# Layer 0's normed input turned to channels through DRAM, as planes of half words, in place of TensorE transposes

## The chip, the cores and the metric

The kernel runs on one core of one Trainium2 chip. A core has five engines that run side by side, each taking its instructions in order: TensorE (PE in the profile, with PEld for its weight loads), VectorE (DVE), ScalarE (ACT), GpSimd (POOL) and SyncE (SP, which here only issues DMAs). The metric is the device time of one execution in microseconds. Before the change it is 2533.7 us, the median of three runs (2533.55 to 2534.89).

## The reference

64 graphs of 256 nodes with 256 features pass two layers. Layer 0 is a gated graph network, layer 1 a graph attention layer:

```python
# layer 0
h = jnp.maximum(_layernorm(x, axis=-1), 0.0)
A = (adj != 0)
for i in range(3):
    m = jnp.einsum('bnd,de->bne', h, weight[i])
    aggr = jnp.einsum('bst,bsd->btd', A, m)
    h = _gru_cell(aggr, h, w_ih, w_hh, b_ih, b_hh)
x = x + h
# layer 1
h = jnp.maximum(_layernorm(x, axis=-1), 0.0)
h = (h @ W.T + b).reshape(B, N, 4, 64)
logits = leaky_relu(l_src[:, :, None, :] + l_dst[:, None, :, :], 0.2)
probs = softmax(where(adj == 1, logits, NEG_INF), axis=2)
x = x + einsum('bijh,bjhc->bihc', probs, h)
```

The change concerns the first line of layer 0 alone: its result is wanted in two layouts, nodes on the partitions (for the aggregation) and channels on the partitions (for the gates).

## The kernel before

The 64 graphs go through in 32 pairs. A pair has 512 rows (two graphs of 256 nodes), kept as four blocks of 128 rows; `x`, `xn` and the adjacency hold rows on the partitions, `hT_a`, the state of the gated network, holds the 256 channels as two blocks of 128 partitions with 512 nodes each.

There is no loop that the hardware schedules. The program is written out by `plan`: `at(tick, phase, p, fn)` files a piece of code under a tick and one of three phases, and at the end all pieces are emitted by tick, then by phase (STEP, READY, REST), and within a phase with the later pair first. Each engine executes its own instructions in that order and waits on semaphores for the others. A piece that stands early in the order and waits holds up everything behind it on its engine.

A pair starts at tick t0 = 18 p. Its three steps of the gated network take six ticks each, at t0 + 0, t0 + 12 and t0 + 24, so that in the steady state each tick has exactly one step piece, from one of three pairs in flight: modulo 18, ticks 0 to 5 belong to the first step of the newest pair, ticks 6 to 11 to the third step of the pair two before, ticks 12 to 17 to the second step of the pair one before. When ticks are numbered below, they are meant modulo 18. The rest, layer normalisation, layer 1, loads and stores, is filled in between as READY and REST pieces. Layer 1 of a pair runs up to tick t0 + 66, so up to four pairs are in work at once.

The pieces of one step that matter here: `tick_3` ends on VectorE with the sum that starts the bank `pe` (L479), `tick_4` has `first_n` (L495), which VectorE writes into the bank `pn0`, and `tick_5` starts with the product that TensorE adds into that bank (`input_n`, L500, recorded at L312). TensorE's product must wait for VectorE's `first_n`.

The input of layer 0 is made like this (times relative to t0):

- `plan_norm` (L329): statistics at -14 and -13, the reciprocal deviation on GpSimd at -13, the normed rows `xn_a` by four VectorE instructions (L351) at -7.
- `plan_relu_T` (L360): at -4 and at -3, four TensorE transposes each (L370) into a bank of PSUM and one ScalarE relu (L371) out of it into `hT_a`.
- `first_hi` and `first_lo` (L740, L744) at -3: the relu of `xn_a` split in a rounded part `hNhi` on ScalarE (L742) and the remainder `hNlo` on VectorE (L746).
- `state_sums` (L401) at -1: differences of `hT_a` on VectorE.

Around these ticks VectorE also has the maxima of layer 1 (L899), the statistics of the second layer normalisation (L339), the shift `top` (L908 to L910) and the last steps' updates (L527, L528), all in the order of the plan. Another DMA transpose is there already: `linked` (L863) brings the mask of layer 1 turned out of DRAM, issued on SP at t0 + 36, behind a write of the same data at t0 + 35 (L803).

Buffers are named by tag in `BUFS`: a tag with n buffers is handed out n times before the first is reused. `row` has four, of which the rows of scores (`drow_0`, `drow_1`, L856) use two per pair; the first four uses are for `hh_T` and two of the message weights.

Of the kernel before, what the change touches and what calls it, by code (L numbers as in the profile page):

```python
# [9 lines left out]
F32 = mybir.dt.float32  # L10
F32R = mybir.dt.float32r
BF16 = mybir.dt.bfloat16
I32 = mybir.dt.int32
AF = mybir.ActivationFunctionType
ALU = mybir.AluOpType
# [2 lines left out]
P = 128  # L18
# [8 lines left out]
def gated_gnn_then_gat_kernel(  # L27
# [39 lines left out]
    nc = tc.nc  # L67
    B, N, D = x.shape
    L = weight.shape[0]
# [3 lines left out]
    KD = D // P  # L73
    KN = N // P
    PB = 2
    R = PB * KN
    T = PB * N
# [10 lines left out]
    dram = ctx.enter_context(tc.tile_pool(name="rows", bufs=2, space=bass.MemoryType.DRAM))  # L88
# [8 lines left out]
    def bank(name):  # L97
        return ps_m.tile([P, 512], F32, tag="mm", name=name)

    BUFS = {  # L100
        "x": 5, "adj": 2, "edge": 2, "noedge": 2, "hT_a": 2, "xn": 2, "val": 2, "row": 4, "zz": 4, "o": 2,
    }

    def buf(tag, shape, name, dtype=F32):
        return sb.tile(shape, dtype, tag=tag, name=name, bufs=BUFS.get(tag, 1))
# [6 lines left out]
    def load_adj(p, name):  # L112
        at = buf("adj", [P, R, N], f"{name}_{p}", I32)
        nc.sync.dma_start(at, adj_rows[ts(p, T), :].rearrange("(r q) t -> q r t", q=P))
        return at
# [10 lines left out]
    def load_gates(name, src):  # L126
        nat = buf("zz", [P, G, D], f"{name}_nat")
        for g0 in range(0, G, 3):
            nc.sync.dma_start(
                nat[:, g0 : g0 + 3, :], src[g0 * P : (g0 + 3) * P, :].rearrange("(g q) d -> q g d", q=P)  # L130
            )
        return nat

    def load_square(tag, name, src):
        y = buf(tag, [P, KD, D], name)
        nc.sync.dma_start(y, src.rearrange("(k q) e -> q k e", q=P))
        return y
# [5 lines left out]
    hh_T = [buf("row", [P, G * P], f"hh_T_{k}") for k in range(KD)]  # L143
    w_msgs = [load_square("Z", "w_msg_0", weight[0])]
    ih_nat = load_gates("ih", w_ih)
    w_msgs += [load_square("row", f"w_msg_{l}", weight[l]) for l in range(1, L)]
    w_nat = load_square("zz", "w_nat", W)
    bi = const.tile([P, G], F32, name="bi")
    bh = const.tile([P, G], F32, name="bh")
# [5 lines left out]
    make_identity(nc, ident)  # L155
    ident16 = const.tile([P, P], BF16, name="ident16")
    nc.vector.tensor_copy(ident16, ident)
# [144 lines left out]
    def flat(y):  # L302
        return y.rearrange("q r d -> q (r d)")
# [17 lines left out]
    STEP, READY, REST = range(3)  # L321
# [4 lines left out]
    def at(tick, phase, p, fn):  # L326
        plan.setdefault(tick, ([], [], []))[phase].append((-p, fn))

    def plan_norm(src, name, p, ticks):  # L329

        v = {}

        def stats(r0):
            def fn():
                if not v:
                    v["st"] = small.tile([P, R, 6], F32, tag="st", name=f"st_{name}")
                    v["mv"] = small.tile([P, R, 2], F32, tag="mv", name=f"mv_{name}")
                for r in (r0, r0 + 1):
                    nc.vector.bn_stats(v["st"][:, r, :], src()[:, r, :])  # L339
                    nc.vector.bn_aggr(v["mv"][:, r, :], v["st"][:, r, :])  # L340
            return fn

        def deviation():
            rstd = v["rstd"] = small.tile([P, R], F32, tag="rstd", name=f"rstd_{name}")
            nc.vector.tensor_scalar_add(rstd, v["mv"][:, :, 1], EPS)
            nc.gpsimd.tensor_tensor(rstd, rstd, mhalf, ALU.pow)

        def result():
            xn = v["xn"] = buf("xn", [P, R, D], f"xn_{name}")
            for r in range(R):  # L350
                nc.vector.tensor_scalar(  # L351
                    xn[:, r, :], src()[:, r, :], v["mv"][:, r, 0:1], v["rstd"][:, r : r + 1],
                    op0=ALU.subtract, op1=ALU.mult,
                )

        for t, fn in zip(ticks, (stats(0), stats(2), deviation, result)):
            at(t, READY, p, fn)
        return v

    def plan_relu_T(v, tag, name, p, ticks):  # L360

        w = {}

        def fn(k):
            def go():
                if not w:
                    w["hT"] = buf(tag, [P, KD, T], f"hT_{name}")
                pt = bank(f"pt_{name}_{k}")
                for r in range(R):
                    nc.tensor.transpose(pt[:, ts(r, P)], v["xn"][:, r, ts(k, P)], ident)  # L370
                nc.scalar.activation(w["hT"][:, k, :], pt, AF.Relu)  # L371
            return go

        for k, t in enumerate(ticks):
            at(t, REST, p, fn(k))
        return w

    def by_c(y):
# [184 lines left out]
    def plan_tail(t0, p, v, g, turn_back, residual):  # L563
# [6 lines left out]
        def links():  # L570
            v["link"] = buf("hNhi", [P, PB, KN, N], f"link_{p}", BF16)
            for i in range(PB):
                pt = ps_m.tile([P, KN, N], BF16, tag="mm", name=f"plink_{p}_{i}")
                for j in range(KN):
                    for s in range(KN):
                        nc.tensor.transpose(pt[:, j, ts(s, P)], v["noedge"][:, i * KN + s, ts(j, P)], ident16)
                nc.vector.tensor_scalar_mul(v["link"][:, i, :, :], pt, 1 / 16)
# [132 lines left out]
    def plan_pair(p):  # L710
        t0 = APART * p
        v = {}
# [3 lines left out]
        def ready(t, fn):  # L716
            at(t0 + t, READY, p, fn)
# [14 lines left out]
            v["edge"] = buf("edge", [P, R, N], f"edge_{p}", F32R)  # L732
            nc.vector.tensor_scalar(v["edge"], v["adj"], 0.0, None, op0=ALU.not_equal)

        xn_a = plan_norm(lambda: v["x"], f"a{p}", p, [t0 - 14, t0 - 13, t0 - 13, t0 - 7])
        ready(-1 if p else -2.5, to_edge)
        h = plan_relu_T(xn_a, "hT_a", f"a{p}", p, [t0 - 4, t0 - 3])


        def first_hi():  # L740
# [37 lines left out]
        for l in range(L):  # L778
            end = last and l == L - 1
            g = Step(f"{p}_{l}", l, lambda: h["hT"], end)  # L780
            t = 2 * SUB * l
# [15 lines left out]
        def bar():  # L797

            v["noedge"] = buf("noedge", [P, R, N], f"noedge_{p}", BF16)
            nc.vector.tensor_scalar(v["noedge"], v["adj"], 1.0, 16 * MASKED, op0=ALU.not_equal, op1=ALU.mult)  # L800
            if not last:
                v["noedge_rows"] = dram.tile([R, P, N], BF16, tag="noedge", name=f"noedge_dram_{p}")
                nc.sync.dma_start(v["noedge_rows"].rearrange("r q t -> q r t"), v["noedge"])  # L803
# [3 lines left out]
        if last:  # L807
            plan_tail(t0, p, v, g, lambda i: turn_back(L - 1, i), residual)
            return
        xn_b = plan_norm(lambda: v["x"], f"b{p}", p, [t0 + 32, t0 + 33, t0 + 33, t0 + 34])  # L810
        hb = plan_relu_T(xn_b, "hT_b", f"b{p}", p, [t0 + 35, t0 + 36])

        def values(r0):
# [37 lines left out]
        rows, drow, logits = {}, {}, {}  # L851
# [11 lines left out]
        def linked():  # L863

            v["link"] = buf("link", [P, KN, T], f"link_{p}", BF16)
            nc.sync.dma_start_transpose(v["link"], v["noedge_rows"].rearrange("r q t -> (r q) t"))
# [59 lines left out]
        for y in range(R * H // 2):  # L926
            r, h0 = divmod(2 * y, H)
# [36 lines left out]
    for p in range(NPAIR):  # L964
        plan_pair(p)
# [52 lines left out]
```

## Time and profile before

| | |
|---|---|
| median of three runs | 2533.7 us |
| the profiled execution | 2540.86 us |
| its span, first to last instruction | 2539.1 us |
| granted TensorE clock, mean | 0.995 |
| period of a pair in the steady state | 76.94 us |
| transposes of `pt_a` (L370) | 256, in 64 groups of four |
| evictions of `pt_a` (L371) | 64, 0.59 us each |
| `xn_a` (L351) | 128 instructions, median 403 ns |
| DMA engines | 251.91 MB moved, mean 99 GB/s |

The page gives busy times and shares of each engine over the span; the chain is the sequence of work that ended last, followed back from the last instruction. A line of the timeline reads: start in us, length in us, engine, source line, operation, output from inputs, shapes, count, and in brackets how long the engine idled before it and who released it. Neighbouring instructions of one engine overlap a little (VectorE's by some 0.08 us), so that the distance between two starts is what an instruction costs its queue. A line of the waits reads: who waited, for whom, us in total, how many times, the longest.

### The profile page before, as it was taken

What the parts mean: (1) busy time and instruction counts of PE and PEld (TensorE: products, weight loads), DVE (VectorE), ACT (ScalarE), POOL (GpSimd) and SP (SyncE); (2) the same over time, 40 slices, a digit from 0 to 9 for tenths busy, and PEclk for the clock granted to TensorE, in tenths of its full rate; (3) what the DMA queues carried; (4) which work ended last, traced back from release to release, by engine and by line L of the source; (5) the groups of instructions that cost most, each with busy time, mean ns of one, the idle gap of its engine ahead of it and who ended that gap; (6) DMA issues with size and microseconds to landing.
All of it is one profiled execution on the core that took longest, in us unless ns stands there. A gap on an engine that the chain in (4) does not pass through costs nothing.

```text
span 2539.1 us, 38539 instructions
## 1 busy us (share of the span) xinstructions
PE 2514.5 (99%) x13918; PEld 2246.4 (88%) x13918; DVE 1824.1 (72%) x4458; ACT 1466.2 (58%) x3095; POOL 645.5 (25%) x514
## 2 busy tenths in 40 slices
PE   8999999999999999999999999999999999999998
PEld 6888898888889888989888988888988889898887
DVE  5567777677777777776777776777777777767667
ACT  3456565565555565555665655655656656556664
POOL 0122232222222222323232323222222223222221
PEclk9999999999999999999999999999999999999998
DMA  3033434553435544345544444534344544354443
GB/s 94 17 74 88 97 93 108 109 125 92 92 92 117 109 113 99 87 95 117 117 100 93 98 102 109 125 92 100 88 113 109 119 95 93 87 124 110 93 95 89
DMA packets 168223, 251.91 MB, mean 99 GB/s; under 512 B 42896, under 2 KB 128352, under 8 KB 168032
## 3 DMA queue, kind: packets, MB, share of 16 engines
q0 software_dynamic: 33728, 130.03, 26.6%
q1 hardware_dynamic: 132736, 119.41, 16.0%
q8 instruction: 110, 1.80, 0.3%
q14 instruction: 81, 0.66, 0.1%
q10 hardware_dynamic: 1568, 0.01, 0.0%
HBM read 215.62 MB, written 25.67 MB: 95 GB/s over the span
## 4 chain that ended last, share of the span: by engine, by line
PE 97%; DVE 1%; DMA 1%; ACT 1%; issue 0%; POOL 0%; SPq 0%; DVEq 0%
PE pd L312 20%; PE pn L312 13%; PE pc L312 13%; PE po L542 9%; PE pa L440 7%; PE qb L418 6%; PE pe L312 6%; PE p L312 6%; PE qa L418 5%; PE pv L820 4%; PE pback L770 3%; PE pt_a L370 1%; PE pt_b L370 1%; PE pc L238 1%; DVE any L899 0%; DMA hh_nat<-in_L_gnn_w_hh_dram 0%
## 5 line engine op out<-in xcount | busy, mean ns | idle before, releaser
L510 POOL TENSOR_TENSOR R<-hT_a,hn 128x512 f32<-128x512 f32 x191 | 317.8, 1664 | 879.4 <-ACT hn L506 821.5
L312 PE MATMUL pn<-aggr,w_a 128*128 128x256 f32 x1536 | 367.1, 382 | 0.0
L312 PE MATMUL pd<-T,w_a 128*128 128x256 f32 x1536 | 366.3, 381 | 0.0
L312 PEld LDWEIGHTS pn<-aggr,w_a 128*128 128x128 f32 x1536 | 287.0, 190 | 43.1 <-DVE pn L495 6.4
L312 PEld LDWEIGHTS pd<-T,w_a 128*128 128x128 f32 x1536 | 287.9, 191 | 37.6
L542 PEld LDWEIGHTS po<-val,zz 128*128 128x128 f32 x2048 | 250.3, 195 | 4.5
L542 PE MATMUL po<-val,zz 128*128 128x65 f32 x2048 | 247.2, 275 | 0.0
L899 DVE CUSTOM_DVE_ANT_0 any<-drow,noedge 128x256 f32<-128x256 f32 x496 | 236.9, 478 | 9.8 <-DMA drow<-score_dram 1.0
L506 ACT ACTIVATE hn<-pn,bi 128x256 f32<-128x256 f32 x384 | 160.3, 469 | 144.3 <-PE pn L312 144.2
L425 ACT ACTIVATE R<-pc,brz 128x256 f32<-128x256 f32 x192 | 80.5, 470 | 278.5 <-PE pc L312 278.5
L527 DVE SCALAR_TENSOR_TENSOR R<-Z,R 128x512 f32<-128x512 f32 x192 | 131.8, 687 | 147.6 <-POOL R L510 142.8
L558 POOL TENSOR_TENSOR x<-x,o 128x256 f32<-128x256 f32 x124 | 112.0, 904 | 481.6 <-DVE o L553 481.6
L761 DVE TENSOR_TENSOR hNlo<-pback,hNhi 128x512 fp32r<-128x512 f32 x128 | 88.4, 691 | 201.6 <-ACT hNhi L760 201.6
L919 ACT ACTIVATE zz<-zz,val 128x256 f32<-128x256 f32 x496 | 224.9, 509 | 0.0
L495 DVE SCALAR_TENSOR_TENSOR pn<-R,hn 128x512 f32<-128x512 f32 x192 | 142.5, 742 | 93.7 <-ACT hn L421 77.2
L425 ACT ACTIVATE R<-pe,brz 128x256 f32<-128x256 f32 x192 | 80.5, 470 | 185.9 <-PE pe L312 185.9
L528 DVE SCALAR_TENSOR_TENSOR hT_a<-R,hn 128x512 f32<-128x512 f32 x192 | 174.6, 909 | 14.3 <-ACT m5n L446 1.4
L312 PE MATMUL pd<-T,w_h 128*128 128x256 f32 x768 | 181.5, 379 | 0.0
L312 PE MATMUL pc<-aggr,w_a 128*128 128x256 f32 x768 | 181.5, 379 | 0.0
L312 PE MATMUL pe<-aggr,w_a 128*128 128x256 f32 x768 | 181.4, 379 | 0.0
L312 PE MATMUL pc<-hT_a,w_h 128*128 128x256 f32 x768 | 181.4, 379 | 0.0
L312 PE MATMUL p<-T,w_a 128*128 128x256 f32 x768 | 181.4, 379 | 0.0
(176 smaller groups left out, 5258.5 us busy)
## 6 DMA issues: line engine op xcount, KB each, us to landing
zz<-score_dram POOLq DMA_DIRECT2D x62, 1024.0 KB, 11.7
zz<-topT_dram POOLq DMA_DIRECT2D x62, 1024.0 KB, 8.7
adj<-in_adj_dram SPq DMA_DIRECT2D x64, 512.0 KB
drow<-score_dram SPq DMA_DIRECT2D x62, 512.0 KB
x<-in_x_dram SPq DMA_DIRECT2D x32, 512.0 KB
out_dram<-x SPq DMA_DIRECT2D x31, 512.0 KB
noedge_dram<-noedge SPq DMA_DIRECT2D x31, 256.0 KB
score_dram<-score SPq DMA_DIRECT2D x124, 4.0 KB
```

The costliest lines, as they stand in the source:

```text
L312: nc.tensor.matmul(pt[:, ts(c, N)], w[:, k, j * D + c * P : j * D + (c + 1) * P], src[:, k, :], start=start and c == 0 and k == 0, stop=(c ...
L418: nc.tensor.matmul(pt, w_n[:, j, :], src, start=start, stop=True, skip_group_check=True)
L425: nc.scalar.activation(of(dst, i)[:, c, :], src[:, c, :], AF.Tanh, bias=brz[:, g0 + c : g0 + c + 1], scale=0.5)
L440: nc.tensor.matmul(pt[:, ts(i, N)], hN[half][:, i * KN + s, ts(e, P)], edge[:, i * KN + s, :], start=(s == 0 and half == 0), stop=(s == KN ...
L495: nc.vector.scalar_tensor_tensor(by_c(self.bank(f"pn{i}")), of(self.R, i), 1.0, of(self.hn, i), op0=ALU.add, op1=ALU.mult)
L506: nc.scalar.activation(n__[:, c, :], p_n[:, c, :], AF.Tanh, bias=bi[:, 2 * KD + c : 2 * KD + c + 1])
L510: nc.gpsimd.tensor_sub(of(self.R, i), of(self.hT(), i), n__)
L527: nc.vector.scalar_tensor_tensor(d_, of(self.Z, i), 1.0, d_, op0=ALU.add, op1=ALU.mult)
L528: nc.vector.scalar_tensor_tensor(of(self.hT(), i), d_, 0.5, of(self.hn, i), op0=ALU.mult, op1=ALU.add)
L542: nc.tensor.matmul(po[:, ts(h_, VC)], zz[:, j, h_, ts(s, P)], v["val"][:, i * KN + j, ts(h_, VC)], start=(j == 0), stop=(j == KN - 1),)
L899: nc.vector.tensor_tensor_reduce(any_, drow[r // KN][:, h, :], v["noedge"][:, r, :], 1.0, -3.0e38, ALU.add, ALU.max, accum_out=v["top"][:, ...
L919: nc.scalar.activation(zz[:, h, :], zz[:, h, :], AF.Prelu, alpha=ALPHA, bias=v["val"][:, r, S0 + H + h : S0 + H + h + 1],)
```

## The change

For pairs 2 to 31 the turned input no longer comes from TensorE. The normed rows are made three ticks earlier (-10 in place of -7) and put through the relu in place by ScalarE. `plan_turn` then takes them to channels in three pieces: `halve` at -9 copies the 32-bit words on VectorE into two planes of 16-bit half words (low halves, high halves, 256 each to a row) and writes them to DRAM; `turn` at -8 reads them back with one DMA transpose[...], so that each plane arrives with channels on the partitions; `join` at -3 puts low and high halves side by side again on VectorE, into `hT_a`. Both DMAs are issued on SP. To make room, the tag `row` goes from four buffers to two, and the message weights of steps 1 and 2 are loaded into the tag `noedge`.

```diff
-        "x": 5, ..., "row": 4, "zz": 4, "o": 2,
+        "x": 5, ..., "row": 2, "zz": 4, "o": 2,
...
-    w_msgs += [load_square("row", f"w_msg_{l}", weight[l]) for l in range(1, L)]
+    w_msgs += [load_square("noedge", f"w_msg_{l}", weight[l]) for l in range(1, L)]
...
+    def plan_turn(src, tag, name, p, ticks):
+        w = {}
+
+        def halve():
+            words = buf("words", [P, R, 2, D], f"words_{name}", U16)
+            nc.vector.tensor_copy(words.rearrange("q r w d -> q r d w"), src().bitcast(U16).rearrange("q r (d w) -> q r d w", w=2))
+            w["rows"] = dram.tile([R, P, 2 * D], U16, tag="words", name=f"words_dram_{name}")
+            nc.sync.dma_start(w["rows"].rearrange("r q e -> q r e"), words.rearrange("q r w d -> q r (w d)"))
+
+        def turn():
+            w["turned"] = buf("turned", [P, 2, KD * T], f"turned_{name}", U16)
+            nc.sync.dma_start_transpose(
+                w["turned"].rearrange("q w (k n) -> q (w k) n", k=KD), w["rows"].rearrange("r q e -> (r q) e")
+            )
+
+        def join():
+            w["hT"] = buf(tag, [P, KD, T], f"hT_{name}")
+            nc.vector.tensor_copy(
+                flat(w["hT"]).bitcast(U16).rearrange("q (n w) -> q n w", w=2), w["turned"].rearrange("q w n -> q n w")
+            )
+
+        at(ticks[0], READY, p, halve)
+        at(ticks[1], REST, p, turn)
+        at(ticks[2], READY, p, join)
+        return w
...
-        xn_a = plan_norm(lambda: v["x"], f"a{p}", p, [t0 - 14, t0 - 13, t0 - 13, t0 - 7])
+        dma_a = p >= 2
+        norm_ticks = (-14, -13, -13, -10) if dma_a else (-14, -13, -13, -7)
+        xn_a = plan_norm(lambda: v["x"], f"a{p}", p, [t0 + t for t in norm_ticks])
         ready(-1 if p else -2.5, to_edge)
-        h = plan_relu_T(xn_a, "hT_a", f"a{p}", p, [t0 - 4, t0 - 3])
+        if dma_a:
+            ready(-10, lambda: nc.scalar.activation(flat(xn_a["xn"]), flat(xn_a["xn"]), AF.Relu))
+            h = plan_turn(lambda: xn_a["xn"], "hT_a", f"a{p}", p, [t0 - 9, t0 - 8, t0 - 3])
+        else:
+            h = plan_relu_T(xn_a, "hT_a", f"a{p}", p, [t0 - 4, t0 - 3])
```

Of the program's order: TensorE loses 60 rows of four transposes and nothing else moves in it; VectorE gets `halve` and `join`, both directly behind the `pe` sum (L479) of their tick, and `xn_a` earlier; ScalarE gets the relu in tick 8 and loses two evictions in ticks 14 and 15; GpSimd's order is unchanged; SP gets the write and the transpose of a pair ahead of the output write of an earlier one.

More of the change, by code (lines that the diff above doesn't have):

```diff
@@ L12 @@
 BF16 = mybir.dt.bfloat16
+U16 = mybir.dt.uint16
 I32 = mybir.dt.int32
@@ L100, in gated_gnn_then_gat_kernel @@
     BUFS = {
-        "x": 5, "adj": 2, "edge": 2, "noedge": 2, "hT_a": 2, "xn": 2, "val": 2, "row": 4, "zz": 4, "o": 2,
+        "x": 5, "adj": 2, "edge": 2, "noedge": 2, "hT_a": 2, "xn": 2, "val": 2, "row": 2, "zz": 4, "o": 2,
     }
```

## The prediction

> **What bounds the kernel now.** I read the page first: busy shares, then the chain that ended last. TensorE is busy for 99% of the span and makes 97% of the chain; the transposes that the change removes stand in that chain with 1%.
>
> ```profile
> PE 2514.5 (99%) x13918; PEld 2246.4 (88%) x13918; DVE 1824.1 (72%) x4458; ACT 1466.2 (58%) x3095; POOL 645.5 (25%) x514
> ...
> PE 97%; DVE 1%; DMA 1%; ACT 1%; issue 0%; POOL 0%; SPq 0%; DVEq 0%
> ```
>
> A share of 72% for VectorE is an average over stages, so I looked next at TensorE's timeline over one steady pair of graphs (its period is 1094.32 - 1017.38 = 76.94 us, and its pattern repeats), around the two groups of L370:
>
> ```profile
> 1054.34 0.60 PE L370 MATMUL pt_a<-ident,xn_a 128*128 128x128 f32 x4
> 1054.78 0.60 PE L770 MATMUL pback<-ident,hT_a 128*128 128x128 f32 x4
> ...
> 1058.67 0.60 PE L370 MATMUL pt_a<-ident,xn_a 128*128 128x128 f32 x4
> 1059.11 0.60 PE L418 MATMUL qb<-T4n,w_n 128*128 128x256 f32 x2
> ...
> 1062.99 0.27 PE L837 MATMUL ptopT<-ident,top 128*16 128x128 f32 x1
> 1063.10 1.98 PE L312 MATMUL pn<-aggr,w_a 128*128 128x256 f32 x8
> ```
>
> A group of four transposes holds TensorE for 0.44 us (start to next start, 1054.78 - 1054.34), not the 0.60 of its own pipelined length. The `pn` product that follows at 1063.10 needs `first_n` (L495) from VectorE. The same stretch on VectorE:
>
> ```profile
> 1046.09 0.18 DVE L551 RECIPROCAL rden<-po 128x4 f32<-128x4 f32 x1 [2.20 <-PE po L542]
> ...
> 1057.56 0.69 DVE L479 TENSOR_TENSOR pe<-pd,m 128x512 f32<-128x512 f32 x1
> 1058.16 0.41 DVE L339 BATCH_NORM_STATS2 st_b<-x 128x6 f32<-128x256 f32 x1
> ...
> 1059.84 0.24 DVE L910 TENSOR_SCALAR top<-top,barred 128x16 f32<-128x16 f32 x1
> 1060.69 1.22 DVE L746 SCALAR_TENSOR_TENSOR hNlo_a<-xn_a,hNhi_a 128x1024 fp32r<-128x1024 f32 x1 [0.61 <-ACT hNhi_a L742]
> 1062.33 0.70 DVE L495 SCALAR_TENSOR_TENSOR pn<-R,hn 128x512 f32<-128x512 f32 x1 [0.42 <-ACT hn L421]
> ```
>
> VectorE waits for TensorE at 1046.09 and then runs without a gap worth the name until 1060: 13.28 of the 14.00 us are busy in the view by stretches, the rest is between instructions. Its only slack before `first_n` is 0.61 + 0.42 us, both waits for ScalarE. `first_n` ends at 1063.03, `pn` starts at 1063.10. The waits of the weight loads say the same for nearly every pair:
>
> ```profile
> PEld pn L312 <- DVE pn L495: 6.4, 30, 0.2
> ```
>
> So in this stretch two engines are bound at once, TensorE and a queue on VectorE that is anchored to the end of the fourth output product at 1045.9. Elsewhere VectorE has room: it idles 5.3 us in 1023 to 1040.
>
> [...] the first pair's `link` transpose (256 KB, issued at 153.93 with nothing beside it) keeps the DMA engines 0.63 busy over 155 to 157, which is 1.26 us or some 208 GB/s. [...] L733 agrees for the first (1024 elements in 676 ns, against 681 ns for the 512 of L404). [...] No instruction in this trace hops so, and the cost of the change turns on it.
>
> **The change part by part.** It touches pairs 2 to 31, 30 of 32.
>
> *TensorE, removed:* 2 groups of 4 transposes a pair, 0.435 us each: 0.87 us a pair, 30 x 0.87 = 26.1 us. All of it is on the bounding engine.
>
> *ScalarE:* 2 evictions of 0.59 us go from ticks 14 and 15; one relu over 1024 columns comes in tick 8 at about 1.06 us (L742 has that shape). In sum nothing, but the place matters. The relu waits for `xn_a`, which VectorE now makes in tick 8, and the exponentials (1.07) and the `hNhi` cast (0.59) are queued behind it.
>
> *VectorE, moved:* `xn_a` (4 instructions, 1.4 us at the 403 ns of one) moves from 1040.36 to 1027.1.
>
> *VectorE, added:* `halve` in tick 9 behind L479, `join` in tick 15 behind L479. Both are copies of 2048 half words, one side of each hopping between two planes. Below: 2048 at L733's rate (0.52 ns each and 0.14 fixed) is 1.2 us. [...] At one element a cycle as in L404: 2.3 us. [...] I take 1.9[...]; 1.2 and 3.7 stay as ends. Nothing below 1.2 is expected[...].
>
> *Place of `halve` (H):* `xn_a` ends at 1028.5, relu 1029.6, exponentials 1030.5, `hNhi` 1031.0 (it ended at 1029.0); `hNlo`, two output instructions and L479 then end at 1032.9, before TensorE wants it at 1033.74. `halve` runs 1032.9 to 1032.9 + H; the state sums, maxima and one output (2.8 us) follow, and `first_n` ends at 1036.3 + H. TensorE wants it at 1038.93, so H up to 2.6 us costs nothing; above, the surplus per pair. At 1.9 it is hidden by the idle time that VectorE had there and by the place that `xn_a` left.
>
> *Place of `join` (J):* the queue from 1058.16 to `top` (1.8 us) now starts after it, so `hNlo_a` can start at 1059.9 + J, `first_n` 1.14 later, and it ends at 1061.8 + J. The waits for ScalarE are gone, since ScalarE loses two evictions and TensorE's inputs to it come 0.4 to 0.9 earlier. `pn` starts at 1061.83 + J instead of 1063.10: a change of J - 1.27 us, and never better than the -0.87 that TensorE saves. Behind `first_n` all follows shifted, as TensorE waits with it, and the 1.17 us that VectorE idles at 1069.35 absorb the remainder. With J = 1.9 this is +0.63 us a pair. It holds for pairs 3 to 31: when pair 2 is prepared, no maxima run yet and VectorE idles 1.50 us at 144.38, so that pair gains 0.87.
>
> *DMA and queues:* a write of 512 KB at 1035 (the output of the same size: issued 1048.03, moved 1049.0 to 1050.5) lands by about 1038; the transpose is twice `link`: issue 2 x 1.24, moving 2 x 1.26, so landed by about 1045, and `join` wants it at 1058. The DMA engines move nothing between 1034 and 1045. On SP both stand ahead of the output write of 1048, which waits for GpSimd anyway; the loads of `x` and `adj` come behind that. Cost nothing, with 13 us to spare. GpSimd's queue has no change.
>
> *`row` from 4 buffers to 2, `w_msg` in `noedge`:* the rows of a pair are loaded at 1088 and last read by the maxima at 1057 of the cycle before; nothing.
>
> Sum: 29 x 0.63 - 0.9 = +17.4 us. The profiled execution took 2540.86 us (span 2539.1 and 1.8 around), 0.28% over the median of 2533.7; the difference is carried to the median unscaled: 2551.
>
> **Rivals.**
> 1. *The join is a plain two-a-cycle copy, the hop free* (J = 1.2). Then 29 x -0.06 - 0.9 = -2.6 us, 2531: the saving on TensorE turns wholly into a wait. For it: L733[...].
> 2. *One element a cycle* (J = H = 2.3): 29 x 1.01 - 0.9 = +28.4, 2562. With the hop besides (3.7): 29 x 2.43, and H beyond 2.6 by 1.1 at the first `pn`, 29 x 1.1: +101.5, 2635.
> 3. *TensorE stays alone in front* (the faster side). Place: `pn` in tick 17 of the schedule. It needs `first_n` no later than TensorE, which is J below 1.27; full 26.1 us come at J = 0.40 (2508). [...] For it: 99% against 72%. Against: the gapless stretch, which a mean over the span hides.
> 4. *The transpose lands late* and VectorE waits at `join`. It needs 13 us more than twice `link`; each microsecond beyond costs 29 us. Nothing in the profile speaks for it but that planes of half words were not moved before.
>
> **How the numbers follow.** This kernel's runs tell a change from none at about 0.2%, 5 us. Forecast (J near 1.9) 0.38; rival 1 0.20, of which 0.15 within 5 us and 0.05 below; rival 2 at 2562 0.20 and at 2635 0.07; rival 3 0.10; rival 4 0.05. Slower 0.70, same 0.15, faster 0.15. The range leaves out rival 3 and the far end of 2 and 4: 2526 to 2590.
>
> **What would show it.** Right: L370 for `pt_a` down from 256 to 16; `join` near 1.9 us on VectorE with no gap before `first_n`; waits of TensorE for `first_n` of about 1.5 us (0.87 + 0.63) in some 29 places; TensorE's busy share lower; no wait at `join` for DMA. Wrong: a gap on VectorE before `first_n`; a `join` of 1.2 us or less; waits of `pn` in tick 10 (then `halve` is too long); a DMA wait at `join`.

## The result and the profile after

The changed kernel takes 2654.8 us (median of four runs, 2649.7 to 2659.0) against 2534.1 for the kernel before: ratio 1.0475, 95% interval 1.0453 to 1.0498. The forecast was 2551 with a range up to 2590, so the sign was right and the size was not: +121 us in place of +17. The execution in the profile took 2659.0 us, its span was 2656.9 and its mean granted clock 0.982 (0.995 before). Runs of one kernel fall into two groups some 6 us apart by the mean clock that they were granted (for the kernel before 0.998 or more, or about 0.995), so differences under 5 us are not read, and "at like clock" below means that only runs of 0.998 or more are compared.

The page of the changed kernel, busy shares and the shares of the chain that ended last:

```profile
PE 2537.9 (96%) x13678; PEld 2249.5 (85%) x13678; DVE 1977.3 (74%) x4518; ACT 1475.2 (56%) x3065; POOL 655.5 (25%) x514
...
PE 58%; DVE 33%; ACT 6%; issue 2%; DMA 1%; POOL 0%; DVEq 0%; SPq 0%; ACTq 0%
```

TensorE executes 240 matmuls fewer and is yet busy for 23 us longer, and VectorE now makes a third of the chain. Both are explained in what follows. The instruction groups of the two new copies (count, then duration in ns as minimum, median, maximum):

```profile
L386 DVE COPY words_a<-xn_a x30: 5372/5604/5629, 122.0 to 2454.9; 128x2048 uint16<-128x2048 uint16 x30
...
L398 DVE COPY hT_a<-turned_a x30: 1216/1218/1220, 147.6 to 2484.7; 128x2048 uint16<-128x2048 uint16 x30
```

Both move 2048 half words per partition. `halve` (L386) reads them in order and writes each to the other plane than the last one: 5.60 us, 2.7 ns each. `join` (L398) reads each from the other plane and writes them in order: 1.22 us, 0.6 ns each. VectorE's timeline in one steady pair shows what 5.6 us do to its queue (`...` marks lines left out):

```profile
1164.08 0.69 DVE L508 TENSOR_TENSOR pe<-pd,m 128x512 f32<-128x512 f32 x1
1164.68 5.61 DVE L386 COPY words_a<-xn_a 128x2048 uint16<-128x2048 uint16 x1
1169.86 0.95 DVE L433 TENSOR_TENSOR T<-hT_a 128x512 f32<-128x512 f32 x1
...
1172.73 0.69 DVE L524 SCALAR_TENSOR_TENSOR pn<-R,hn 128x512 f32<-128x512 f32 x1
```

There is no bracket of idle time on any of these lines: VectorE runs through, and the `pn` of tick 11 (L524) ends at 1173.42. TensorE's timeline, first around `pn` of tick 17 of the pair before, behind `join`, then around this `pn`:

```profile
1117.15 0.27 PE L873 MATMUL ptopT<-ident,top 128*16 128x128 f32 x1
1118.04 1.99 PE L313 MATMUL pn<-aggr,w_a 128*128 128x256 f32 x8 [0.61 <-DVE pn L524]
...
1169.09 1.90 PE L571 MATMUL po<-val,zz 128*128 128x65 f32 x16
1173.48 3.06 PE L313 MATMUL pn<-aggr,w_a 128*128 128x256 f32 x8 [2.50 <-DVE pn L524]
1176.34 2.55 PE L313 MATMUL pd<-T,w_a 128*128 128x256 f32 x8
1178.72 1.89 PE L313 MATMUL pn<-aggr,w_a 128*128 128x256 f32 x8
```

TensorE waits 2.50 us in tick 11 and 0.61 in tick 17. After the long wait the same eight products that take 1.89 us at 1178.72 take 3.06 and 2.55. The granted clock shows why. All its changes in this trace lie on one grid of 3.41 us, so the stretches below are cut at the lines of that grid (length, busy time with counts of PE, PEld, DVE, ACT and POOL, then the granted TensorE clock, the DMA share, GB/s). The first three hold this wait and what follows it; the last two hold another one, which ended at 1336.05 and whose `pn` took 1.99 us:

```profile
1170.83:1174.25 3.42, 0.93 (x6) 0.71 (x6) 3.35 (x11) 0.20 (x1) 1.11 (x1) 1.00 0.45 153
1174.25:1177.66 3.41, 3.41 (x10) 2.66 (x9) 2.97 (x11) 1.55 (x4) 1.20 (x2) 0.50 0.78 154
1177.66:1181.07 3.41, 3.41 (x21) 3.07 (x19) 0.00 (x0) 1.26 (x4) 1.17 (x1) 1.00 0.00 0
...
1331.26:1334.67 3.41, 2.26 (x19) 2.07 (x17) 3.38 (x7) 0.84 (x2) 0.00 (x0) 1.00 0.25 86
1334.67:1338.09 3.42, 2.04 (x9) 1.82 (x10) 3.25 (x13) 0.91 (x2) 1.10 (x1) 1.00 0.47 116
```

After the wait the clock that TensorE is granted is halved for one stretch of 3.41 us. That costs 3.41 x 0.50 = 1.7 us in this pair, and it is how TensorE can be busy for longer with less work. It does not follow each wait: of the 30 products in tick 11, 10 took 1.99 us, the others 2.44 to 3.78. The place of the wait on the grid divides the two kinds. Of the 28 waits of 2.5 us, those that began 0.66 to 1.15 us ahead of a grid line, ten in all, left the clock alone: they are split between two stretches, as in the last two lines. All 18 others lowered it, most of them by leaving one stretch nearly idle, as in the first line. The two earliest waits, of 3.4 and 4.2 us, lowered it too. No run moves a wait along the grid on purpose, so this is read from the traces and not tested.

The waits over the whole span (us in total, times, longest):

```profile
PEld pn L313 <- DVE pn L524: 112.1, 61, 4.6
PE pn L313 <- DVE pn L524: 95.4, 59, 4.2
```

Before, the first of these lines read 6.4 us in 30 places. From these readings the theory to be tested: the scattered writes of `halve` make TensorE wait (30 x 2.5 = 75 us), the clock that falls after it costs 1.7 us in 20 of 30 places, 34 us, and the waits behind `join` (29 of about 0.6 us) use up what TensorE saves. The rivals are that VectorE has simply got too much work, and that the added DMA traffic does it.

### The profile page after: what moved, and what is told of

Its sections match the earlier page's. It is cut to its first block, busy times and chain, and to the rows that moved or that the text cites. A ratio compares the mean times of both kernels' runs of the same rounds, so it can differ in the third digit from the quotient of the medians.

```text
span 2656.9 us, 38099 instructions
## 1 busy us (share of the span) xinstructions
PE 2537.9 (96%) x13678; PEld 2249.5 (85%) x13678; DVE 1977.3 (74%) x4518; ACT 1475.2 (56%) x3065; POOL 655.5 (25%) x514
## 4 chain that ended last, share of the span: by engine, by line
PE 58%; DVE 33%; ACT 6%; issue 2%; DMA 1%; POOL 0%; DVEq 0%; SPq 0%; ACTq 0%
PE pn L313 14%; PE pd L313 11%; PE pc L313 7%; DVE words_a L386 6%; PE pa L469 5%; PE pv L856 4%; PE qa L447 3%; PE po L571 3%; PE qb L447 3%; DVE any L935 3%; PE pe L313 2%; PE p L313 2%; ACT zz L970 2%; DVE hT_a L557 2%; DVE hNlo L797 2%
## 5 line engine op out<-in xcount | busy, mean ns | idle before, releaser
L313 PE MATMUL pn<-aggr,w_a 128*128 128x256 f32 x1536 | 390.3, 399 | 95.4 <-DVE pn L524 95.4
L313 PEld LDWEIGHTS pn<-aggr,w_a 128*128 128x128 f32 x1536 | 297.3, 197 | 152.4 <-DVE pn L524 112.1
L313 PE MATMUL pd<-T,w_a 128*128 128x256 f32 x1536 | 381.6, 393 | 0.0
L313 PEld LDWEIGHTS pd<-T,w_a 128*128 128x128 f32 x1536 | 301.9, 200 | 44.5
L587 POOL TENSOR_TENSOR x<-x,o 128x256 f32<-128x256 f32 x124 | 122.8, 991 | 575.0 <-DVE o L582 575.0
L524 DVE SCALAR_TENSOR_TENSOR pn<-R,hn 128x512 f32<-128x512 f32 x192 | 133.7, 696 | 68.7 <-ACT hn L450 55.4
```

The lines of the kernel that those rows point to most:

```text
L313: nc.tensor.matmul(pt[:, ts(c, N)], w[:, k, j * D + c * P : j * D + (c + 1) * P], src[:, k, :], start=start and c == 0 and k == 0, stop=(c ...
L524: nc.vector.scalar_tensor_tensor(by_c(self.bank(f"pn{i}")), of(self.R, i), 1.0, of(self.hn, i), op0=ALU.add, op1=ALU.mult)
```

## The experiments

Each experiment starts from the changed kernel. Where nothing else is said, it computes the same. The kernel before took 2534.8 (median) beside the first eight of them and 2536.6 beside the last.

| run | median us | ratio to before, 95% interval | clock in the profile |
|---|---|---|---|
| the change | 2654.8 | 1.0475 (1.0453 to 1.0498) | 0.982 |
| e1_dense_write | 2539.1 | 1.0006 (0.9997 to 1.0015) | 0.995 |
| e6_far_planes | 2656.8 | one run | 0.980 |
| e4_warm | 2620.9 | 1.0337 (1.0319 to 1.0356) | 0.999 |
| e5_split | 2576.2 | 1.0161 (1.0144 to 1.0178) | 0.998 |
| e3_late_join | 2668.1 | 1.0520 (1.0489 to 1.0550) | 0.972 |
| e8_warm_late | 2615.3 | 1.0310 (1.0290 to 1.0330) | 0.998 |
| e2_dense_late | 2522.1 | 0.9948 (0.9929 to 0.9967) | 0.999 |
| e7_dense_mid | 2529.2 | 0.9975 (0.9963 to 0.9987) | 0.995 |
| e9_noedge_first | 2508.4 | 0.9890 (0.9872 to 0.9907) | 0.996 |

**The same copy, written densely.** Only the order in which `halve` walks over the elements changes: all low halves of a row, then all high halves. Source, destination, bytes, DMAs and place in the queue stay.

```diff
-nc.vector.tensor_copy(words.rearrange("q r w d -> q r d w"), src().bitcast(U16).rearrange("q r (d w) -> q r d w", w=2))
+nc.vector.tensor_copy(words, src().bitcast(U16).rearrange("q r (d w) -> q r w d", w=2))
```

> halve goes through its elements plane by plane: it reads every second half word and writes densely, where the changed kernel reads densely and writes every half word into the other plane. All else as in the changed kernel, DMA traffic and the relu too. Theory (the copy's scattered writes are the cost): halve falls from 5.60 us to about join's 1.22, which reads scattered and writes densely; the stall of pn in tick 11 goes, the clock stays at 0.995, and what is left is the wait behind join (0.78 us a pair, from 117.26 to 118.04 in one pair) against the 0.87 saved on TensorE: 29 x -0.09, about 2531 us. Rival (DMA traffic, or the relu in front of the exponentials): halve shorter, but the time stays above 2600.

The group of `halve`:

```profile
L386 DVE COPY words_a<-xn_a x30: 1217/1387/1391, 122.1 to 2339.8; 128x2048 uint16<-128x2048 uint16 x30
```

and the wait for `pn` in the view of the waits:

```profile
PE pn L313 <- DVE pn L524: 17.9, 29, 0.7
```

5.60 us become 1.39, the 2.5 us waits are gone, the clock is back at 0.995, and 116 of the 121 us with them. At like clock, too, it is level with the kernel before (2532.3 against 2534.5). The 29 waits that stay, 17.9 us, are those behind `join`. Since both DMAs are still there, they are not the cause: that rival falls.

**Is it the distance of the planes?** The two planes lie 2 KB apart in place of 512 bytes; the write to DRAM goes out in two pieces.

```diff
-words = buf("words", [P, R, 2, D], f"words_{name}", U16)
+words = buf("words", [P, 2, R, D], f"words_{name}", U16)
...
+for h in range(2):
+    nc.sync.dma_start(w["rows"].rearrange("r q (w d) -> w q r d", w=2)[h], words[:, h, :, :])
```

> `halve` writes half words scattered as in the changed kernel, but the two planes lie far apart (2 KB) so that the step between successive half words of a plane and the pattern of the write differ; the words go out in two DMAs. Theory (a scattered write of half words costs 2.7 ns each, wherever it goes): `halve` takes 5.6 us again and the time is about 2655. Rival (it is [...] the distance between planes, that costs): `halve` takes 1.2 to 2.6 us and the time is about 2540.

```profile
L386 DVE COPY words_a<-xn_a x30: 5329/5559/5635, 120.7 to 2451.5; 128x2048 uint16<-128x2048 uint16 x30
```

That group line of the run says 5.56 us, and the time is 2656.8: between 512 bytes and 2 KB the distance makes no difference. `join` reads across the same 2 KB and took 1.22 us. Whether it is the jump that costs, or that each half word is written by itself, was not separated: no run writes half words apart without alternating between two places.

**What the fallen clock is worth.** Twenty transposes of the identity (added work, their result is not used) fill TensorE's wait in tick 11.

```diff
 self.first_n(1)
+if self.l == L - 1 and not self.end:
+    pt = bank(f"warm_{self.n_}")
+    for j in range(20):
+        nc.tensor.transpose(pt[:, ts(j % 4, P)], ident, ident)
 self.input_n(0)
```

> In the third step of each pair but the last, 20 transposes of the identity into a bank that nobody reads (0.109 us each, 2.2 us) stand ahead of the pn product of tick 11, where TensorE waits 2.6 us in the changed kernel. They add work and take no wait away. Theory (the wait lets the granted clock fall, and the next 5 us run slow, some 1.2 us a pair in the mean, 0.013 of the span): clock back to 0.995, pn and pd at 1.89 us again, 2655 - 35 = about 2620. Rival (the slow products behind the wait come from something else, such as VectorE's copy or the DMA beside them): clock unchanged, 2655 or more.

TensorE's timeline of this run at the same place:

```profile
1152.89 2.35 PE L546 MATMUL warm<-ident 128*128 128x128 f32 x20
1155.55 1.99 PE L313 MATMUL pn<-aggr,w_a 128*128 128x256 f32 x8 [0.30 <-DVE pn L524]
1157.38 1.89 PE L313 MATMUL pd<-T,w_a 128*128 128x256 f32 x8
```

`pn` still comes when VectorE lets it, but the products behind it run at 1.99 and 1.89 and the clock is 0.999. 2654.8 - 2620.9 = 33.9 us: that is the price of the fallen clock, apart from the wait. It agrees with 20 x 1.7 = 34 us from the trace.

**Place or load?** `halve` in four blocks with scattered writes, spread over ticks 9, 10 and 11. VectorE's work is no less (2022 us busy against 1977), only its place is another.

```diff
-at(ticks[0], READY, p, halve)
+for r, t in enumerate((0, 1, 2, 2)):
+    at(ticks[0] + t, READY, p, piece(r))
+at(ticks[0] + 2, READY, p, store)
```

> halve cut into its four blocks of rows, each a copy with the same scattered writes (1.4 us each, 5.6 in sum): one in tick 9, one in tick 10, two in tick 11; write and transpose follow in tick 11. Theory (what counts is the place in VectorE's queue before a first_n, not VectorE's load): no block is longer than the 2.6 us of room before pn in tick 11, the stall there goes, clock 0.995, and the time is that of the dense write, about 2531. Rival (VectorE's total load decides): VectorE busy as in the changed kernel (1977 us), and the time stays above 2600.

It landed between the two: 2576.2. VectorE's timeline shows the two blocks of tick 11:

```profile
1056.01 4.34 DVE L388 COPY words_a<-xn_a 128x512 uint16<-128x512 uint16 x2
...
1061.96 0.17 DVE L591 RECIPROCAL rden<-po 128x4 f32<-128x4 f32 x1
```

and the waits name new victims:

```profile
PE pn L313 <- DVE pn L535: 26.7, 31, 1.2
...
PE qb L458 <- DVE qb L493: 15.9, 29, 1.6
```

The long waits in tick 11 are gone, with the fallen clock. But the last two blocks took 4.34 us (GpSimd's update of the states ran from 1056.65 beside them), and TensorE's fourth output product, which before made VectorE wait for it at the like of 1061.96, now finds VectorE late. The stretch without gaps up to tick 17 then starts late, and `qb` waits in 29 places; this last link is read from the order of the lines and not tested by itself. So more work on VectorE cost 79 us less than the same work at one place; some 34 of them are the clock's, by the price that e4_warm gives it. The load rival falls, and my expectation of level time falls too: the room in ticks 9 to 11 was not as large as 5.6 us.

**A later join alone.** `join` at tick t0-1, behind both `pn` of tick 17.

```diff
-h = plan_turn(lambda: xn_a["xn"], "hT_a", f"a{p}", p, [t0 - 9, t0 - 8, t0 - 3])
+h = plan_turn(lambda: xn_a["xn"], "hT_a", f"a{p}", p, [t0 - 9, t0 - 8, t0 - 1])
```

> join at t0 - 1 in place of t0 - 3, behind both first_n of its step, all else as in the changed kernel, halve slow. Theory: the wait of pn in tick 17 (0.78 us a pair) goes, 29 x 0.78 = 23 us: about 2632; the wait of pn in tick 11 stays. Rival (the wait for first_n merely moves to another piece, or join is wanted before): within 5 us of the changed kernel's 2655.

Not as expected: 2668, slower than the change itself. TensorE's timeline has the wait in tick 17 gone (1128.40), but more of the long waits are followed by half the speed throughout (3.78 for 1.89), and the scores of layer 1 wait (18.6 us in 17 places; the line shown is the longest):

```profile
580.74 0.27 PE L873 MATMUL pscore<-ident,score 128*32 128x128 f32 x1 [4.10 <-DVE score L863]
...
697.72 3.78 PE L313 MATMUL pn<-aggr,w_a 128*128 128x256 f32 x8 [2.49 <-DVE pn L524]
...
1128.40 1.93 PE L313 MATMUL pn<-aggr,w_a 128*128 128x256 f32 x8
```

Two things are mixed here, so the same edit was run together with the transposes of e4_warm, which held the clock at 0.999 there:

```diff
-h = plan_turn(lambda: xn_a["xn"], "hT_a", f"a{p}", p, [t0 - 9, t0 - 8, t0 - 3])
+h = plan_turn(lambda: xn_a["xn"], "hT_a", f"a{p}", p, [t0 - 9, t0 - 8, t0 - 1])
...
+    for j in range(20):
+        nc.tensor.transpose(pt[:, ts(j % 4, P)], ident, ident)
```

> The scattered write of the changed kernel, with the join at t0-1 and, as added work, the 20 transposes of the identity that fill TensorE's wait in tick 11. The late join alone came out slower than the changed kernel (2668 against 2655) at a clock of 0.972, although its wait at `pn` of tick 17 had gone. Theory (the late join does gain its 0.78 us per pair, and the lower clock alone hid it): clock 0.995 or above, and 2621 - 29 x 0.78 = about 2598. Rival (the late join has a price of its own, the late scores at `pscore`, 18.6 and 17.4 us of waits): clock 0.995 or above and yet 2615 to 2635.

2615.3: at the edge of the rival's range. The clock is 0.998, the waits at `pn` fall from the 27.9 us of e4_warm (57 places) to 11.5, and a part of the gain comes back as waits at the scores:

```profile
PE pn L313 <- DVE pn L524: 11.5, 30, 2.0
PE pscore L877 <- DVE score L867: 8.6, 11, 1.9
```

So the late join gains some 6 us of the 23 expected, little more than what is read here (at like clock 2608.2 and 2612.4 against 2617.5 and 2618.1). Its loss without the transposes (+13) came from the clock: leaving out the first and last 100 us, the trace of the late join has 123 us at half the clock, that of the changed kernel 75, since ten of its waits halved it for two stretches of the grid and not only for one, against two waits in the changed kernel. By the reading of the grid above this is a matter of where the waits came to lie on it, which nothing in the edit aims at; no run tests that by itself.

**Dense write and late join together.**

```diff
-nc.vector.tensor_copy(words.rearrange("q r w d -> q r d w"), src().bitcast(U16).rearrange("q r (d w) -> q r d w", w=2))
+nc.vector.tensor_copy(words, src().bitcast(U16).rearrange("q r (d w) -> q r w d", w=2))
...
-h = plan_turn(lambda: xn_a["xn"], "hT_a", f"a{p}", p, [t0 - 9, t0 - 8, t0 - 3])
+h = plan_turn(lambda: xn_a["xn"], "hT_a", f"a{p}", p, [t0 - 9, t0 - 8, t0 - 1])
```

> `halve` writes the two planes one after the other (dense writes, scattered reads), and the rows after the transpose are joined at tick t0-1 of the next pair in place of t0-3, behind `pn` of tick 17. The late join alone took the wait of `pn` in tick 17 away, the dense write alone took the wait in tick 11 and the clock's fall away and landed level with the kernel before (2539). Theory (what is left of the join's price is its wait at `pn` of tick 17, about 0.6 to 0.8 us per pair, and TensorE's saved 0.87 us per pair then comes through): both together 2539 - 29 x 0.8 = about 2515 us, the clock at 0.995 or above, no wait at `pn`. Rival (the late join moves the stall to the scores of the next pair, as 17 waits of `pscore` with the late join alone hinted): 2530 to 2540, with the waits at `pscore` in the place of those at `pn`.

2522.1: faster than before, and 7 us short of the expectation. The waits at `pn` have left the list. What is left is `pscore`, and the waits of ScalarE name where it starts:

```profile
ACT zz L908 <- DMA link<-noedge_dram: 54.9, 29, 3.2
...
PE pscore L873 <- DVE score L863: 8.1, 15, 1.4
```

With the dense write and `join` at t0-3 the first line read 2.7 us in 4 places. The timelines of VectorE and GpSimd with the late join:

```profile
679.86 1.21 DVE L398 COPY hT_a<-turned_a 128x2048 uint16<-128x2048 uint16 x1
...
683.11 1.47 POOL L539 TENSOR_TENSOR R<-hT_a,hn 128x512 f32<-128x512 f32 x1 [0.91 <-ACT hn L535]
683.34 1.79 DVE L836 TENSOR_SCALAR noedge<-adj 128x1024 bf16<-128x1024 int32 x1
```

The mask `noedge` stands behind the join in the queue. Pushed back by 1.2 us it meets GpSimd's update (683.11 to 684.58) and takes 1.79 us in place of 0.67. An estimate from these lines, that the mask does its 0.67 us only when the update has ended, gives 684.58 + 0.67 = 685.25 against the measured end of 685.13; why it would wait was not shown. By the order of the queues the mask's write to DRAM and the `link` transpose then follow late, ScalarE waits for `link` with the `hNhi` cast queued behind it, and VectorE's score waits for that cast. The last experiment tests this.

**The join between the two `pn`.** To e2_dense_late:

```diff
-h = plan_turn(lambda: xn_a["xn"], "hT_a", f"a{p}", p, [t0 - 9, t0 - 8, t0 - 1])
+h = plan_turn(lambda: xn_a["xn"], "hT_a", f"a{p}", p, [t0 - 9, t0 - 8, t0 - 2])
```

> Dense write, and the join at tick t0-2: by the order of VectorE's queue it then stands behind the first `pn` of tick 17 and ahead of the second (with `xn_b` between), where at t0-3 it stood ahead of both and at t0-1 behind both. Theory (what the join costs is decided by whether a `pn` stands behind it in the queue, not by its 1.22 us): the second `pn` comes late in place of the first, by 0.3 to 0.7 us per pair, and the time lies between the two others, 2525 to 2536, with PE's waits at `pn` back at 29. Rival (the second `pn` has slack, and only the first one must not be behind the join): no waits at `pn`, and without the late start of the scores of the next pair 2515 to 2522.

2529.2 as median, with the widest spread of all (22 runs, 2521.0 to 2539.8). Neither theory holds whole: the waits at `pn` did not come back (the rival's part), but the median is not the rival's. ScalarE waits for `link` for 15.6 us in 8 places. It beats the kernel before by 0.25%. At like clock (2521.0 to 2525.6) it is level with the join at t0-1 (2519.4 to 2527.5).

**The mask ahead of the join.** To e2_dense_late, `noedge` is made ahead of the second `pn` of tick 17.

```diff
-ready(28 if last else 35, bar)
+ready(28 if last else 34.99, bar)
```

> Dense write and join at t0-1, and besides the mask `noedge` (L836) is made right ahead of the second `pn` of tick 17, where with the late join it was made behind the join, 1.79 us long beside GpSimd's update, and its write to DRAM and the `link` transpose came late: ScalarE then waited for `link` 29 times, 54.9 us in sum (2.7 with the join at t0-3), and the scores 8.1 us for that at `pscore`. Theory (the late `link` is what was left of the late join's price): waits for `link` back below 10 us, none at `pscore`, and 2522 - 29 x 0.3 to 0.45 = 2509 to 2514. Rival (VectorE's queue in ticks 17 to 18 has no room left for 0.68 us ahead of `pn`): the second `pn` waits 0.1 to 0.5 us in some 29 places and the time is 2520 to 2535.

2508.4, with the waits for `link` back down and the mask at 0.67 us:

```profile
ACT zz L908 <- DMA link<-noedge_dram: 2.3, 4, 0.8
```

```profile
L836 DVE TENSOR_SCALAR noedge<-adj x32: 670/671/687, 148.6 to 2451.0; 128x1024 bf16<-128x1024 int32 x32
```

`pn` is gone from TensorE's list of waits and `pscore` is there with one wait of 0.8 us, as before the change; the chain on the page is TensorE's again:

```profile
PE 2488.8 (99%) x13678; PEld 2222.0 (88%) x13678; DVE 1881.5 (75%) x4518; ACT 1469.6 (58%) x3065; POOL 628.7 (25%) x514
...
PE 96%; DVE 2%; ACT 1%; DMA 1%; issue 0%; POOL 0%; SPq 0%; DVEq 0%; ACTq 0%
```

This version is 1.1% faster than the kernel before (0.9872 to 0.9907), with VectorE busy for 57 us more than there and TensorE for 26 us less (2488.8 against 2514.5).

## Why the prediction was wrong

*TensorE, 26.1 us saved:* right, and all of it is to be had. e9_noedge_first is 26 us under the kernel before at like clock (2507.9 against 2533.8), its pairs take 76.03 us in place of 76.95 (from the `ptopT` product of one to that of the next), and 2508 is also the figure that rival 3 gave for the full saving.

*`halve` at 1.9 us:* the step that failed. The prediction gave both copies one price, "one side of each hopping between two planes", and one pair of ends, 1.2 and 3.7. Measured: 1.22 where the hop is on the side that is read, 5.60 where it is on the side that is written, beyond the upper end. No trace or run stood behind the 1.9 or the upper end. The lines measured before were L733, 1024 elements in 676 ns (what the prediction calls two a cycle), and L404, 512 in 681 ns (one a cycle); for 2048 half words they give 1.2 and 2.3 us, and neither shows what a hop costs. A half word that is written to the other plane took 2.7 ns. e1_dense_write changed nothing but that order and gave back 116 of the 121 us; e6_far_planes showed 5.56 us at another distance.

*Place of `halve`, free up to 2.6 us and the surplus per pair above:* right in kind and near in size. At 5.60 it gives a delay of 3.0 us. A steady pair whose clock did not fall took 79.6 us, in e1_dense_write 76.87, so the delay was 2.7 and the room 2.9. e1_dense_write, at 1.39, shows it free.

*Place of `join`, J - 1.27 a pair:* right for this place. At J = 1.22 it says -0.05 us a pair, that is the saving turned wholly into a wait, as in rival 1 (2531). e1_dense_write, where nothing else costs, has pairs of 76.87 us against 76.95 before, and waits 17.9 us in 29 places. It was not a law of the change, only of tick 17: e9_noedge_first has the join elsewhere and no such wait.

*DMA and queues at nothing:* right. No wait for the transpose at `join` appears in the changed kernel, and e1_dense_write pays nothing for both DMAs.

*What the sum did not have:* the granted clock, which it put at nothing without a word. This is the second step that failed. With the measured copies put into the prediction's own sum, 29 x (1.22 - 1.27) + 29 x (5.60 - 2.6) - 0.9 = +84.7, or 2619 us; with the clock held up, e4_warm took 2620.9. The part for `halve` holds as well: the last pair of e4_warm starts 84.6 us later than that of e1_dense_write (2568.1 against 2483.5), where the sum has 29 x 3.0 = 87. The clock's 33.9 us on top make 2652.6 of the measured 2654.8. The prediction priced a wait of TensorE at its length alone. In the trace of the changed kernel all stretches at half the clock begin on one grid of 3.41 us, and waits of 2.5 us lowered the clock in 18 of 28 places.

*Rivals:* rival 2 had the mechanism of `halve` beyond its room, and with its 3.7 us reached 2635; it needed the writing side at 5.6. Rival 1 was right for `join`, in cost (1.22 for its 1.2) and in effect. Rival 4, the late transpose, did not occur for the new transpose. It did occur for the old one, `link`, when the join was moved.

Left open: why a wait's place on the grid decides as it does, and which property of the scattered write makes it slow.

## What to carry to other kernels

When a copy splits or joins interleaved half words, let the side that is written run densely and let the side that is read do the jumping (here 1.39 us in place of 5.60 for the same 2048 half words); price both sides apart. Price a wait of the bounding engine by its length and by what its clock does afterwards (here 33.9 us in all), and test the second by filling the gap. An instruction that is put into a queue moves everything behind it, so after each move look at which engine waits longer for whom, down to the transfers that start from the shifted instructions: here a copy of 1.2 us cost, by the distance to the best version at like clock, 24.4 us at one place (2532.3 - 2507.9), 13.5 at the next (2521.4 - 2507.9), and nothing that shows once the mask stood ahead of it.

## What the hardware showed that was not expected

- Half words written alternately to two places cost 2.7 ns each (5604 ns for 2048; 5559 with the places 2 KB apart in place of 512 bytes). Read alternately from two places they cost 0.6 ns (1218 ns for 2048).
- Waits of 2.5 us halved TensorE's granted clock in 18 of 28 places, each time for one stretch of 3.41 us, twice for two: with two longer waits 33.9 us in all. Every stretch at half the clock begins on one grid of 3.41 us, and the ten waits that left the clock alone all began 0.66 to 1.15 us ahead of a line of that grid. After waits of about 0.6 us (29 in e1_dense_write) no fall shows: the longest single `pn` product of that run took 0.48 us, that of the changed kernel 0.80.
